# Placing the deferred layer-norm steps in ScalarE's order by a count of operands, in a two-layer graph kernel

## The chip, the cores and the metric

The kernel runs on one core of one Trainium2 chip. The metric is the device time of one execution in microseconds (us). The kernel before the change took 1790.8 us, the median of three runs (1789.74 to 1793.45); the execution that was profiled has a span of 1790.1 us.

In the text PE is TensorE (matrix products), DVE is VectorE, ACT is ScalarE, POOL is GpSimd, and SP is the engine whose queue issues the DMA transfers. [...]

## What is computed

There are 16 batches of a 1024 x 128 matrix x, one 1024 x 1024 matrix adj, and 128 x 128 (or 128 x 256) weights, all in float32. Two layers follow one another; each ends with a residual sum and a layer norm over the last axis.

```python
def layer0(x):                                  # a graph convolution
    return layernorm(x + adj @ (x @ w0) + b0)

def layer1(x):                                  # five steps of a gated graph network
    h = x
    for _ in range(5):
        m  = adj @ h                            # in and out matrix are both adj
        av = concat(m, m)
        u3 = h @ u3_w.T + u3_b
        z  = sigmoid(av @ w3_w.T + w3_b + u3)
        r  = sigmoid(av @ w4_w.T + w4_b + u3)
        hv = tanh(av @ w5_w.T + w5_b + (r * h) @ u5_w.T + u5_b)
        h  = (1 - z) * h + z * hv
    return layernorm(x + h)
```

Since both halves of `av` are the same, the two halves of each of w3, w4 and w5 are added once, and the sum is used as one 128 x 128 weight. These sums are the "weight sums" of the change.

## The kernel before

The batches are taken in four groups (q = 0 to 3) of four (k = 0 to 3). For each group, and in layer 1 for each of the five steps s, `aggregate` forms adj times the group by a two-level scheme of Strassen's kind (Winograd's form): seven outer products, each made of seven inner ones. The outer products are worked through in four **chains**, named after the outer products in them: 12, 3, 67 and 54. Chains 12, 67 and 54 handle two outer products side by side (two operands; `len(ns) == 2`), chain 3 only one. Every chain runs through its seven inner products in the order 1, 5, 6, 2, 7, 3, 4 (chain 54: 1, 5, 6, 2, 7, 3 first half, 4, 3 second half). After each inner product the result is taken out of PSUM by ACT or DVE:

```python
after = {
    1: lambda: nc.scalar.copy(fb, fa),               # pa -> pb, on ACT; product 6 goes on in pb
    5: lambda: nc.scalar.copy(x22, fc),
    6: lambda: nc.scalar.copy(x12, fb),
    2: lambda: nc.scalar.copy(x11, fa),
    7: lambda: nc.vector.tensor_add(x22, fb, x22),   # on DVE
    3: lambda: nc.vector.tensor_add(x12, fc, x12),
    4: lambda: nc.scalar.copy(x21, fb),
}
bank_of = {1: pa, 2: pa, 5: pc, 3: pc, 6: pb, 7: pb, 4: pb}
for item in order:
    for hook in hooks.get(item, ()):                 # other work, placed before this product
        hook()
    ...                                              # the matmuls of product a
    with tc.high_priority(), behind_closing():
        after[a]()
    drain(3 if len(ns) == 2 else 1)                  # L392
```

A layer norm takes its statistics on DVE, `rstd` and `shift` on POOL, and applies them on ACT, eight instructions of 128 x 128 for one batch. Those eight, and the transfer that stores the result, are not issued at once but put in a list. `drain` takes them off the list, after the inner products:

```python
def layernorm(y, tag, store, now=False):
    ...
    # 8 x bn_stats and 8 x bn_aggr on DVE                                  L246, L248
    nc.gpsimd.tensor_scalar(rstd, mv[:, :, 1], EPS, None, ALU.add)        # L251
    nc.gpsimd.tensor_tensor(rstd, rstd, power[:, :n], ALU.pow)            # L252
    nc.gpsimd.tensor_tensor(shift, mv[:, :, 0], rstd, ALU.mult)           # L253
    nc.gpsimd.tensor_scalar(shift, shift, -1.0, None, ALU.mult)           # L254

    def apply(c):
        return nc.scalar.activation(y[:, c, :], y[:, c, :], AF.Identity,  # L257
                                    bias=shift[:, c : c + 1], scale=rstd[:, c : c + 1])
    def put():
        nc.sync.dma_start(store, y)                                       # L263
    ...
    for c in range(n):
        waiting.append((slot[0], lambda c=c: tc.keep_in_program_order(apply(c))))
    waiting.append((slot[0], put))

waiting = deque()
slot = [0]

def drain(n, age=3):
    slot[0] += 1
    while waiting and n > 0 and slot[0] - waiting[0][0] >= age:
        waiting.popleft()[1]()
        n -= 1
```

Instructions under `tc.keep_in_program_order` keep the place in which the program states them; others are ordered by the compiler's scheduler, those under `tc.high_priority()` as early as they are ready there.

Layer norms arise in two places. In layer 0 the four norms of group q arise in chain 12 of the next aggregate, where `project(q, k, y)` multiplies the aggregate by w0. It first has ACT fill two PSUM tiles, `seeded`, with the bias (L448, kept in program order), then 16 matmul records per half on PE (L451), then the residual on DVE:

```python
def projections(q):
    room = rooms[q % 2]
    ys = [ypad[0], ypad[1], room[:, 2], room[:, 3]]
    for k in (2, 3):
        nc.sync.dma_start(ys[k], x_rows(q * QUAD + k))
    # before products 5, 2, 3 of chain 12, and at its end
    return {a: [call(project, q, k, ys[k])] for k, a in enumerate((5, 2, 3, "end"))}
```

At the end of chain 67, `fetch` flushes the list and loads the next group into the same buffers; the first sums over the next group (`ahead`) are placed at product 7 of chain 54. In group 1 the weight sums of layer 1 are placed at product 4 of chain 54:

```python
def fetch(q=q):
    drain(99, 0)
    for k in range(2):
        nc.sync.dma_start(ypad[k], x_rows(q * QUAD + k))
    if q + 1 < NQ:
        load(q + 1, rooms[(q + 1) % 2], x_rows)
    else:
        load(0, rows, saved_rows)
    ...
hooks.setdefault(67, {})["end"] = [fetch]
hooks[54] = {7: [call(ahead, rooms[(q + 1) % 2])]}
if q == 1:
    hooks[54][4] = [layer1_weights]
```

The first aggregate of layer 1 carries the projections of group 3 in the same way, with a flush before product 3 of chain 67 (`call(drain, 99, 0)`).

In layer 1 the closing norm of batch k of group q is taken in step k + 1 of group q + 1: `close` is placed before product 6 of chain 54 and works in the tile `hvs` (called `spare`). The next step's `next_load`, before product 1 of chain 3, loads other data into that tile. Chain 54 is followed at once by the **gates** (sigmoid, tanh, update), which need ACT for four instructions of 128 x 512 per unit. There are 12 such closings; the four batches of the last group are finished in `ending`, which flushes the list (`drain(99, 0)`) before each batch.

Of the kernel before, what the change touches and what calls it, by code (L numbers as in the profile page):

```python
# [20 lines left out]
def kernel(  # L21
# [73 lines left out]
    def bank(name, i=None):  # L95
        if i is None:
            i = turns[0]
            turns[0] = (i + 1) % 3
        return ps_m.tile([P, HALF], F32, tag=f"g{i}", name=name)
# [15 lines left out]
    def x_rows(b):  # L115
        return x[b].rearrange("(p c) d -> p (c d)", c=C)
# [91 lines left out]
    def layer0_weights():  # L208
        nc.sync.dma_start(w0_sb, w0)
        nc.sync.dma_start(b0_bc, bass.AP(tensor=b0.tensor, offset=b0.offset, ap=[[0, P], [1, D]]))  # L210

    raw_of = {
        "w3": (w3_w, hvs[:, 0, : 2 * D]), "w4": (w4_w, hvs[:, 0, 2 * D :]),
        "w5": (w5_w, hvs[:, 1, : 2 * D]), "u3": (u3_w, hvs[:, 1, 2 * D : 3 * D]),
        "u5": (u5_w, hvs[:, 1, 3 * D :]),
    }
# [7 lines left out]
    def layer1_weights():  # L224


        tc.keep_in_program_order(nc.vector.tensor_add(bz, bias[:, 0:1], bias[:, 3:4]))
        tc.keep_in_program_order(nc.vector.tensor_add(br, bias[:, 1:2], bias[:, 3:4]))
        tc.keep_in_program_order(nc.vector.tensor_add(bh, bias[:, 2:3], bias[:, 4:5]))
        for name, (w, raw) in raw_of.items():  # L230
            if w.shape[1] == 2 * D:
                tc.keep_in_program_order(
                    nc.vector.tensor_add(raw[:, :D], raw[:, :D], raw[:, D : 2 * D])
                )
            pt = bank(f"pt_{name}")
            tc.keep_in_program_order(nc.tensor.transpose(pt[:, :P], raw[:, :D], ident))
            nc.vector.tensor_copy(w_t[name], pt[:, :P])
# [46 lines left out]
    waiting = deque()  # L284
    slot = [0]

    def drain(n, age=3):
        slot[0] += 1
        while waiting and n > 0 and slot[0] - waiting[0][0] >= age:
            waiting.popleft()[1]()  # L290
            n -= 1
# [9 lines left out]
    def blocks_of(src, ns):  # L301

        if ns in ((1, 2), (3,)):
            v = src.rearrange("p b (h j x) -> p b h j x", h=2, j=2)
            if ns == (1, 2):
                return lambda j, k: v[:, k, :, j]
            return lambda j, k: v[:, 2 + k, 1:2, j]
        at = {(6, 7): slice(1, 3), (5, 4): slice(0, 4, 3)}[ns]
        return lambda j, k: tsum[:, at, k, ts(j, QT)]

    def sums_of(src, ns, pinned=False):
        t = inner[0 if ns in ((1, 2), (6, 7)) else 1]
        for op in inner_sums(blocks_of(src, ns), [t[:, i, : len(ns)] for i in range(4)]):
            if pinned:
                tc.keep_in_program_order(op)
        return op
# [16 lines left out]
    def behind_closing():  # L333

        return tc.issue_after(closed[0].ins) if closed[0] else nullcontext()

    def chain(tag, src, turned, ns, results, hooks, order=(1, 5, 6, 2, 7, 3, 4)):

        xs = blocks_of(src, ns)
        t = inner[0 if ns in ((1, 2), (6, 7)) else 1]
        w = len(ns) * QT
        right = {
            1: xs(0, 0), 2: xs(1, 0), 3: xs(1, 1), 4: t[:, 3], 5: t[:, 0], 6: t[:, 1], 7: t[:, 2],
        }

        def chunk(a, o, c):
            form = "p (d c) -> p c d" if turned else "p (c d) -> p c d"
            return right[a][:, o].rearrange(form, c=2)[:, c]  # L350

        def flat(t):
            return t[:, :w].rearrange("p (o q) -> p o q", o=len(ns))

        pa = ps_m.tile([P, HALF], F32, tag="a", name=f"pa_{tag}")
        pc = ps_m.tile([P, HALF], F32, tag="c", name=f"pc_{tag}")
        fa, fb, fc = flat(pa), flat(pb), flat(pc)

        x11, x12, x21, x22 = results(0, 0), results(0, 1), results(1, 0), results(1, 1)
        after = {  # L360
            1: lambda: nc.scalar.copy(fb, fa),  # L361
# [3 lines that stand above are left out]
            7: lambda: nc.vector.tensor_add(x22, fb, x22),  # L365
# [5 lines that stand above are left out]
            for hook in hooks.get(item, ()):  # L371
                hook()
            a, part = item if isinstance(item, tuple) else (item, range(len(ns)))
            for o in part:
                n = ns[o]
                for c in range(2):
                    product = nc.tensor.matmul(  # L377
                        bank_of[a][:, ts(o, QT)], chunk(a, o, c), left[n][a][:, c, :],
                        start=(a in (1, 5) and o == 0 and c == 0), stop=(c == 1),
                        skip_group_check=True,  # L380
                    )

                    if turned and a in (5, 6, 2) and ns in ((1, 2), (3,)) and o == c == 0:
                        tc.keep_in_program_order(product)

                    if item != a or (ns == (5, 4) and a == 4):
                        tc.keep_in_program_order(product)
            if o < len(ns) - 1:
                continue
            with tc.high_priority(), behind_closing():  # L390
                after[a]()
            drain(3 if len(ns) == 2 else 1)  # L392
        for hook in hooks.get("end", ()):
            hook()

# [234 lines left out]
    def call(f, *args):  # L630
        return lambda: f(*args)
# [9 lines that stand above are left out]
# [11 lines left out]
    for q in range(NQ):  # L652
        room = rooms[q % 2]
        hooks = {}
        if q == 0:
            hooks[12] = {
                5: [turn_rest],
                6: [outer_left, call(sums_of, rows, (3,))],
                7: [call(outer_sums, rows), call(inner_left, 6), call(inner_left, 7)],
            }  # L660
            hooks[67] = {1: [call(inner_left, 5), call(inner_left, 4)]}
            layer0_weights()
            with tc.issue_after(last_left.ins):
                sums_of(rows, (1, 2))
        else:
            hooks[12] = projections(q - 1)
            hooks[12][6] = [call(sums_of, room, (3,)), call(outer_sums, room, False, True)]
# [9 lines that stand above are left out]
            if q == 0:  # L677
                load_layer1_weights()

        def ahead(room):  # L680
            sums_of(room, (1, 2))
            outer_sums(room, True, False)

        hooks.setdefault(67, {})["end"] = [fetch]
        hooks[54] = {7: [call(ahead, rooms[(q + 1) % 2])]}
        if q == 1:
            hooks[54][4] = [layer1_weights]
        if q == 0:
            with tc.issue_after(last_left.ins):
                aggregate(f"x{q}", room, hooks, False)  # L690
        else:
            aggregate(f"x{q}", room, hooks, False)
# [71 lines left out]
    for q in range(NQ):  # L764
        for s in range(STEPS):
            tag = f"{q}_{s}"
            if s == 0:
                if q == 0:
                    hooks = {
                        12: projections(NQ - 1),  # L770
                        3: {5: [call(to_hidden, 0)], 2: [call(to_hidden, 1)]},
                        67: {
                            3: [call(drain, 99, 0), call(to_hidden, 2)],
                            "end": [call(to_hidden, 3)],
                        },
                        54: {},
                    }
                    hooks[12][6] = [call(sums_of, rows, (3,)), call(outer_sums, rows, False, True)]
                else:
                    outer_sums(rows)  # L780
                    hooks = {54: {}}
            else:
                hooks = {54: {}}
# [96 lines left out]
```

## Time and profile before

| what | value |
|---|---|
| time, median of three runs | 1790.8 us |
| span of the profiled execution | 1790.1 us |
| PE busy | 1768.5 us |
| DVE busy | 1309.0 us |
| ACT busy | 789.9 us |
| POOL busy | 94.3 us |
| one apply of a norm on ACT (128 x 128), median | 482 to 487 ns; 7 in a row take 2.80 us |
| ACT copy of a two-operand inner product (128 x 512) | 0.57 to 0.59 us |
| ACT copy of a one-operand inner product (128 x 256) | 0.37 us |
| `rstd` by `pow` on POOL (L252), median | 1.67 us |
| store of a normalized batch, issue to landing, median | 2.6 to 3.3 us |
| load of a batch, issue to landing, median | 3.6 to 4.1 us |

Groups of instructions are written as line, engine, operation, output<-inputs, shape, count, then busy time, mean of one and idle time of the engine ahead of them with what ended it ("<-"). In the timeline each row is a start, a length, an engine and an instruction; idle time ahead of it stands in brackets. A row in which PE is idle names what it waited for. In the table of stretches of time, each row gives the stretch, its length, the busy time of every engine with the number of instructions, the mean granted PE clock (1.00 is full speed), and the share and rate of the DMA engines.

### The profile page before, as it was taken

To read this page: it belongs to the slowest core of one execution; us is meant where nothing else is said; L and a number is where in the kernel's file an instruction comes from. 1 tells how busy PE (TensorE), PEld (TensorE's weight loads), DVE (VectorE), ACT (ScalarE), POOL (GpSimd) and SP (SyncE) were. 2 spreads that over 40 slices of the span, in tenths; PEclk is the share of its full clock that TensorE was granted. 3 is DMA by queue.
4 is the path that set the end of the run, shared out by engine and by line. 5 is a ranking of instruction groups with operands and counts; after the bars stand their busy time and mean duration, and the time that the engine had idled before them with its cause. 6 is when DMAs were issued, how large, how long until landed. Compare 5 with 4: busy or idle time off the path is not lost.

```text
span 1790.1 us, 19915 instructions
## 1 busy us (share of the span) xinstructions
PE 1768.5 (99%) x6709; PEld 1267.6 (71%) x6709; DVE 1309.0 (73%) x2280; ACT 789.9 (44%) x1418; POOL 94.3 (5%) x142
## 2 busy tenths in 40 slices
PE   8999999999999999999999999999999999999998
PEld 7788885857668586775857667585775857667584
DVE  7977786676767757777777857777777577777777
ACT  2345555253443534435253443534435253453536
POOL 0112220000000000000000000000000000000004
PEclk9999999999999999999999999999999999999999
DMA  6232344331414415252442415234143231514222
GB/s 226 71 118 106 130 114 96 74 85 33 112 30 94 118 36 118 56 133 57 97 97 92 106 36 118 71 86 115 52 114 106 48 80 50 118 36 95 71 71 94
DMA packets 404212, 159.25 MB, mean 89 GB/s; under 512 B 388240, under 2 KB 389136, under 8 KB 404112
## 3 DMA queue, kind: packets, MB, share of 16 engines
q1 hardware_dynamic: 403248, 154.84, 33.8%
q10 hardware_dynamic: 864, 3.15, 0.4%
q8 instruction: 54, 0.88, 0.2%
q14 instruction: 46, 0.38, 0.1%
HBM read 92.93 MB, written 65.01 MB: 88 GB/s over the span
## 4 chain that ended last, share of the span: by engine, by line
PE 93%; DVE 3%; POOL 1%; ACT 1%; issue 1%; DMA 0%; SPq 0%; DVEq 0%; POOLq 0%
PE pb L377 23%; PE pa L377 13%; PE pc L377 13%; PE ph L517 8%; PE pu L476 8%; PE pu L494 8%; PE seeded L509 8%; PE ph L518 8%; PE pa_x L377 2%; PE pc_x L377 2%; PE seeded L451 1%; POOL rstd L252 1%; ACT ypad L257 0%; DMA rows<-in_x_dram 0%; DVE stats L246 0%
## 5 line engine op out<-in xcount | busy, mean ns | idle before, releaser
L377 PE MATMUL pb<-e,inner 128*128 128x256 f32 x864 | 206.8, 380 | 3.0 <-ACT pb L361 3.0
L533 DVE TENSOR_TENSOR tsum<-tsum,hid 128x512 f32<-128x512 f32 x158 | 108.8, 689 | 107.7 <-ACT tsum L528 107.6
L377 PEld LDWEIGHTS pb<-e,inner 128*128 128x128 f32 x864 | 167.7, 195 | 23.1 <-ACT pb L361 5.0
L528 ACT ACTIVATE tsum<-ph,bh 128x512 f32<-128x512 f32 x158 | 108.5, 687 | 165.4 <-PE ph L518 165.4
L517 PE MATMUL ph<-agg,w_t 128*128 128x512 f32 x320 | 164.7, 596 | 0.0
L494 PE MATMUL pu<-agg,w_t 128*128 128x512 f32 x320 | 164.4, 595 | 0.1
L509 PE MATMUL seeded<-agg,w_t 128*128 128x512 f32 x320 | 163.5, 592 | 0.0
L518 PE MATMUL ph<-tsum,u_t 128*128 128x512 f32 x320 | 163.5, 592 | 0.0
L476 PE MATMUL pu<-hid,u_t 128*128 128x512 f32 x320 | 157.1, 592 | 0.0
L377 PE MATMUL pb<-s,inner 128*128 128x256 f32 x576 | 148.5, 381 | 0.2 <-DVE agg L365 0.2
L377 PE MATMUL pb<-a,inner 128*128 128x256 f32 x576 | 145.4, 381 | 0.0
L504 DVE TENSOR_TENSOR tsum<-tsum,hid 128x512 f32<-128x512 f32 x160 | 110.4, 690 | 46.4 <-ACT tsum L497 46.4
L497 ACT ACTIVATE tsum<-pu,br 128x512 f32<-128x512 f32 x160 | 109.8, 686 | 62.6 <-PE pu L494 62.6
L377 PE MATMUL pc<-e,inner 128*128 128x256 f32 x560 | 134.1, 379 | 0.0
L377 PEld LDWEIGHTS pb<-s,inner 128*128 128x128 f32 x576 | 110.3, 195 | 24.4 <-issue 9.9
L377 PEld LDWEIGHTS pb<-a,inner 128*128 128x128 f32 x576 | 112.3, 196 | 12.1
L512 ACT ACTIVATE tsum<-seeded,bz 128x512 f32<-128x512 f32 x160 | 109.7, 685 | 24.1 <-PE seeded L509 24.1
L377 PEld LDWEIGHTS pc<-e,inner 128*128 128x128 f32 x560 | 109.4, 196 | 11.7 <-issue 0.2
L517 PEld LDWEIGHTS ph<-agg,w_t 128*128 128x128 f32 x320 | 59.8, 190 | 78.2 <-issue 69.0
L518 PEld LDWEIGHTS ph<-tsum,u_t 128*128 128x128 f32 x320 | 61.0, 190 | 76.4 <-issue 57.5
L476 PEld LDWEIGHTS pu<-hid,u_t 128*128 128x128 f32 x320 | 61.0, 191 | 73.4 <-issue 72.3
L534 DVE TENSOR_TENSOR tsum<-tsum 128x512 f32<-128x512 f32 x158 | 109.2, 691 | 5.0
(180 smaller groups left out, 2855.9 us busy)
## 6 DMA issues: line engine op xcount, KB each, us to landing
turned<-ypad SPq DMA_DIRECT2D x48, 512.0 KB, 3.8
rows<-turned SPq DMA_DIRECT2D x192, 128.0 KB, 2.8
hvs<-saved SPq DMA_DIRECT2D x24, 512.0 KB, 3.9
rows<-saved SPq DMA_DIRECT2D x20, 512.0 KB, 4.1
hid<-hidden SPq DMA_DIRECT2D x64, 128.0 KB, 3.3
turned<-ypad SPq DMA_DIRECT2D x32, 256.0 KB, 2.9
rows<-turned SPq DMA_DIRECT2D x128, 64.0 KB, 2.1
hid<-in_x_dram SPq DMA_DIRECT2D x12, 512.0 KB, 3.9
```

Source lines behind the costliest of these rows:

```text
L377: product = nc.tensor.matmul(bank_of[a][:, ts(o, QT)], chunk(a, o, c), left[n][a][:, c, :], start=(a in (1, 5) and o == 0 and c == 0), sto ...
L476: in_order(nc.tensor.matmul(pu, w_t["u3"], hid[:, k, ts(h, HALF)], start=True, stop=True, skip_group_check=True))
L494: in_order(nc.tensor.matmul(pu, w_t["w4"], agg[:, k, cols], start=False, stop=True, skip_group_check=True))
L497: pin(nc.scalar.activation(rh[:, cols], pu, AF.Sigmoid, bias=br))
L504: pin(nc.vector.tensor_mul(rh[:, cols], rh[:, cols], hid[:, k, cols]))
L509: in_order(nc.tensor.matmul(pz, w_t["w3"], agg[:, k, cols], start=False, stop=True, skip_group_check=True))
L512: pin(nc.scalar.activation(z_of[k % 2][:, cols], pz, AF.Sigmoid, bias=bz))
L517: in_order(nc.tensor.matmul(ph, w_t["w5"], agg[:, k, cols], start=True, stop=False))
L518: in_order(nc.tensor.matmul(ph, w_t["u5"], rh_of[k % 2][:, cols], start=False, stop=True))
L528: pin(nc.scalar.activation(hv, ph, AF.Tanh, bias=bh))
L533: pinned(nc.vector.tensor_sub(hv, hv, hid[:, k, cols]))
L534: pinned(nc.vector.tensor_mul(hv, hv, z_of[k % 2][:, cols]))
```

## The change

Three things change. First, the age of a waiting step is counted in operands and not in calls: a product of a chain with two operands counts two, of chain 3 one, and a flush counts nothing. A step has to be fourteen behind its norm (seven products with two operands) and not three calls. Second, at most two steps are placed after a product with two operands, and not three; chain 3 keeps one. Both are meant to keep ACT from standing at a step whose `shift` POOL has not delivered, and from serving several steps ahead of a PSUM copy. Third, the weight sums on DVE are separated from the transposes that turn the weights on PE and placed earlier in chain 54, at its product 5, so that PE finds them done when it turns the weights at product 4.

```diff
-        for name, (w, raw) in raw_of.items():
+        for w, raw in raw_of.values():
             if w.shape[1] == 2 * D:
                 tc.keep_in_program_order(
                     nc.vector.tensor_add(raw[:, :D], raw[:, :D], raw[:, D : 2 * D])
                 )
+
+    def turn_weights():
+        for name, (_, raw) in raw_of.items():
             pt = bank(f"pt_{name}")
             tc.keep_in_program_order(nc.tensor.transpose(pt[:, :P], raw[:, :D], ident))
             nc.vector.tensor_copy(w_t[name], pt[:, :P])
...
-    def drain(n, age=3):
-        slot[0] += 1
+    def drain(n, age=14, time=0):
+        slot[0] += time
         while waiting and n > 0 and slot[0] - waiting[0][0] >= age:
             waiting.popleft()[1]()
             n -= 1
...
-            drain(3 if len(ns) == 2 else 1)
+            drain(2 if len(ns) == 2 else 1, time=len(ns))
...
         if q == 1:
-            hooks[54][4] = [layer1_weights]
+            hooks[54][5] = [layer1_weights]
+            hooks[54][4] = [turn_weights]
```

No instruction is added or removed; only places in the order change.

## The prediction

> **What bounds the kernel now.** I began with the page's busy times and its groups.
>
> ```profile
> PE 1768.5 (99%) x6709; PEld 1267.6 (71%) x6709; DVE 1309.0 (73%) x2280; ACT 789.9 (44%) x1418; POOL 94.3 (5%) x142
> PE 93%; DVE 3%; POOL 1%; ACT 1%; issue 1%; DMA 0%; SPq 0%; DVEq 0%; POOLq 0%
> ```
>
> PE is busy for all but 21.6 us of 1790.1, and the chain that ended last runs through PE for 93% of the span. A change that moves no PE work can win only PE's idle time and whatever PE loses by running slowly. So the ceiling comes first. I compared the starts of successive matmul records with the usual distance for their shape (216 ns for 128x256, 429 ns for 128x512, about 118 ns for 128x128, each the commonest in this trace). Added over the span, PE is late by some 30 us. About 15 of these lie in the first 60 us, ahead of any norm and out of reach. The last 8 us, after PE's last matmul, are out of reach too.
>
> Next I asked what ended ACT's idle time (columns: who <- for whom, total us, times, longest).
>
> ```profile
> ACT hvs L257 <- POOL shift L254: 18.0, 6, 3.1
> ACT ypad L257 <- POOL shift L254: 4.5, 4, 2.9
> ACT rows L257 <- POOL shift L254: 3.2, 1, 3.2
> ACT ypad L257 <- DVE stats L246: 2.6, 1, 2.6
> ```
>
> ACT stands at applies (L257) whose `shift` is not ready: an age of three products is too little, since POOL needs some 2.5 us more after DVE's statistics (75.83 to 78.42 us for one norm in the chain of waits). Whether PE suffers is seen only where it happens. In the timeline of group 1, chain 12 going over into chain 3:
>
> ```profile
> 84.89 0.58 ACT L367 COPY first<-pb 128x512 f32<-128x512 f32 x1 [2.21 <-PE pb L377]
> 88.35 0.49 ACT L257 ACTIVATE ypad<-ypad,shift,rstd 128x128 f32<-128x128 f32 x1 [2.88 <-POOL shift L254]
> 88.75 0.36 ACT L361 COPY pb<-pa_x 128x256 f32<-128x256 f32 x1
> 89.16 1.13 PE L377 MATMUL pb<-e,inner 128*128 128x256 f32 x4 [2.58 <-ACT pb L361]
> ```
>
> One apply waits 2.88 us for POOL; the copy that the next product in pb needs is placed behind it; PE is idle 2.58 us. In group 2 six applies stand ahead of the bias fill of `seeded`:
>
> ```profile
> 137.72 2.42 ACT L257 ACTIVATE ypad<-ypad,shift,rstd 128x128 f32<-128x128 f32 x6 [2.55 <-DVE stats L246]
> 140.05 1.08 ACT L448 COPY seeded<-b_bc 128x512 f32<-128x512 f32 x2
> 140.67 3.00 PE L451 MATMUL seeded<-w_sb,agg 128*128 128x128 f32 x16 [1.81 <-ACT seeded L448]
> ```
>
> Both gaps cost twice, as the table by stretches shows in its clock column (third from the right):
>
> ```profile
> 86.50:90.00 3.50, 0.92 (x5) 0.77 (x5) 3.44 (x9) 1.65 (x5) 3.17 (x5) 1.00 0.38 132
> 90.00:94.00 4.00, 4.00 (x21) 3.85 (x20) 0.69 (x1) 2.87 (x7) 1.92 (x3) 0.57 0.00 0
> 138.50:140.50 2.00, 0.37 (x2) 0.00 (x0) 1.75 (x4) 2.00 (x6) 1.26 (x2) 1.00 0.00 0
> 140.50:145.00 4.50, 4.33 (x20) 4.06 (x21) 1.91 (x6) 1.45 (x4) 1.73 (x3) 0.63 0.29 117
> ```
>
> After each gap PE is busy throughout, but at a clock of 0.57 and 0.63. The trace has the clock at one half for 3.41 us from 90.5 and again from 141.7, and at full speed everywhere else between 15 us and the end. Each costs half of 3.41, 1.7 us, which the busy times do not show.
>
> [...]
>
> **The change part by part.** I went through the list by hand for a layer-0 group with both rules (a two-operand product gives 2 counts, chain 3 gives 1).
>
> *Layer 0, age.* Before, the first applies of the norm made ahead of product 5 come at product 2 of the same chain, two products later. After, seven two-operand products must pass, and no apply is left in chain 12 at all: the first comes at product 5 of chain 3, when `shift` has been ready for over 10 us. So both gaps shown go, with their slow clock: group 1, 2.58 + 1.7 = 4.3 us; group 2, 1.81 + 1.7 = 3.5 us. Small delays beside them (0.2 to 0.3 us per group, after copies that applies held up) bring 0.5. In group 3 and in the first aggregate of layer 1 the six applies ahead of `seeded` cost PE about 0.5 us each, and a copy of pb behind three applies another 0.25 us: 1.5 together. Sum: 9.8 us.
>
> *At most two.* A two-operand product lasts 8 x 0.216 = 1.73 us. Three applies at 0.40 (2.80 us for seven) and a copy of 0.58 are 1.8 us; two are 1.4 us, so ACT keeps up. That is a safeguard; I count nothing for it.
>
> *Closings of layer 1.* Now the eight applies fall into the last three products of chain 54 and the first gates. In the trace of one of them ACT goes through 3 + 3 + 2 applies between sigmoids from 741.7 to 746.0, and PE's product at L517 starts 0.14 us late, and 0.10 us more passes before its next record. Over the 12 closings I find 0.17 to 0.25 us each that ACT causes: about 2.4 us. After, the steps become due at product 5 of the next chain 12, where ACT has 1.73 us per product for 1.4 us of work. The six waits of ACT for POOL (18.0 us) vanish as well, but they hardly held up PE and bring nothing more. Part of the delays (0.19 us in six closings) is DVE's, which still makes the statistics there; it stays.
>
> *Weight sums.* At 118.6 to 121.6 DVE adds the halves just ahead of each transpose; PE idles 0.58 us for the third and is late by about 1 us in all. Placed at product 5 the sums, three times 0.28 us plus three small ones, fit into DVE's idle 0.72 us at 113.5. Gain 0.8 us, once.
>
> Gain in sum: 9.8 + 2.4 + 0.8 = 13.0 us.
>
> **What it can cost.** Fewer steps per product and a later start mean that the list isn't empty when `fetch` comes: by my count 16 entries are left (14 applies, 2 stores), where before there were none; in layer 1's first aggregate the forced flush meets 20 (17 applies) and before 2. Fourteen applies take 5.6 us of ACT. They can be overtaken by the high-priority copies (88.75 above is such an overtaking), so that a copy waits for one apply at most, 0.48 us, and PE has a whole product, 1.73 us less a 0.58 us copy, to spare. But the last store, issued at 107.4 us before, moves to about 109.9 + 5.6 + three copies of 0.58 = 117 us. The load into the same buffer waits for it: [...] The trace shows this wait:
>
> ```profile
> 107.42 0.33 SPq L263 DMA_DIRECT2D saved<-rows  x1
> 110.86 0.33 SPq L113 DMA_DIRECT2D rows<-in_x_dram  x1
> 114.25 1.23 DVE L326 TENSOR_TENSOR tsum<-rows 128x1024 f32<-128x1024 f32 x1 [0.72 <-DMA rows<-in_x_dram]
> ```
>
> Store to load 3.4 us, load to first use 3.4 us. After, the load would land near 124 us instead of 114. PE doesn't need these rows before chain 3, some 20 us further on; but DVE takes its instructions in order, and in chain 12 it is full (20.01 us busy of the 21.00 from 69 to 90, 20.26 of 24.00 from 124 to 148). I estimate 0.5 to 1 us of new PE waits at each of the four seams: 3 us. Net: 13.0 - 3 = 10 us.
>
> **Rivals.** (1) *The load becomes the wait.* If the scheduler leaves L326 where it is in DVE's order, DVE stands up to 10 us, the sums for product 5 of chain 12 come late, and PE loses perhaps 6 us and 1.7 us of slow clock in each of three groups: 23 us, and a time of about 1800. Against it: DVE's order follows the scheduler's own forecast of when the load lands, and that forecast was only 0.7 us off at 114.25. (2) *DVE becomes the bound in chain 12.* With ACT's waits gone, PE needs about 20.7 us there (12 for seven products, 8.6 for four projections of 2.15), DVE 20. Then the gap of group 2 closes only in part: a net gain of some 6 us, 1785. (3) *Everything hidden.* The late stores and loads cost nothing: 1790.8 - 13 = 1778. (4) *The end.* The last closing's applies are now flushed into the gates of `ending`, 3.2 us in one lump ahead of tanh; PE can go on for about two products of 0.86 us in free PSUM banks there, so up to 1 us is lost.
>
> **Range and chances.** 1780.7 us is the sum. Below, the ceiling of 13 us and a run-to-run spread of some 2 us give 1776. Above, the second rival and part of the first give 1788.5. Faster by over 2% needs 36 us, more than PE's late time within reach; I give it 0.01. Slower by over 2% needs the first rival to be worse than estimated: 0.02.
>
> **What would show it.** Right: no apply between 69 and 90 us and in the later chains 12 of layer 0; PE's waits for `pb L361` and `seeded L448` gone; the clock at 1.00 throughout after 15 us; ACT's waits for `shift` near zero except at the end; 14 applies bunched after chain 67; PE's idle for `hvs L233` gone. Wrong: a new row of DVE waiting for `rows<-in_x_dram` or `rows<-saved` of over 2 us with a PE gap behind it; a half-speed stretch at a new place; closings in chain 12 that hold up the copy of pb, so that the steps of layer 1 get longer than the 76.6 us they take without a closing.

## The result and the profile after

The changed kernel takes 1778.5 us, the median of six runs (1777.9 to 1779.3), against 1792.1 us for the one before in the same number of runs (1789.0 to 1794.8). The ratio is 0.9924, with a 95% interval of 0.9911 to 0.9937: 13.6 us, or 0.8%, faster. Beside a later repetition of the changed kernel (1778.5 us) the kernel before took 1790.4 us, so the gain there was 11.9 us, and it is known to about 2 us. The prediction was 1780.7 us. The profiled execution has a span of 1776.1 us.

The page of the changed kernel, its rows of busy time and of the chain that ended last:

```profile
PE 1760.3 (99%) x6709; PEld 1263.2 (71%) x6709; DVE 1308.0 (74%) x2280; ACT 794.3 (45%) x1418; POOL 99.0 (6%) x142
PE 94%; DVE 3%; DMA 1%; POOL 0%; SPq 0%; issue 0%; ACT 0%; DVEq 0%
```

The counts are the same; only the order differs. PE is busy 8.2 us less for the same 6709 matmul records. That is not less work. In the two groups of layer 0 that held the half-speed stretches it is 4.5 us, of which the clock makes 3.4: at half speed the starts of 128x256 records lie 427 ns apart (before, from 143.9 us) and not 216, and the records count as busy throughout (3.42 of 3.42 us from 90.47 us on, at a clock of 0.50). Another 3.1 us lie in layer 1 between 775 and 1697 us, where the clock was full in both kernels. There records only started a little late, and a record of 128x512 lasts 0.59 us at a usual distance of 0.43 us, so that a short delay does not show as idle time. PE's idle time fell from 21.6 us to 15.8 us.

ACT's waits for POOL in the changed kernel (who <- for whom, total us, times, longest), where before there were three such rows with 25.7 us:

```profile
ACT rows L260 <- POOL shift L257: 3.2, 1, 3.2
```

The single wait left is the last norm of the kernel. (Lines are shifted: L257 before is L260 after, L448 is L451; in the kernels below with a list of ages L448 is L454.) In the timeline of ACT at the seam of chains 12 and 3 of group 1, which held the gap of 2.58 us before, the bias fill and the copy now come at once, and the first apply stands at product 5 of chain 3, as counted:

```profile
83.82 0.58 ACT L370 COPY first<-pb 128x512 f32<-128x512 f32 x1 [5.33 <-PE pb L380]
84.30 1.11 ACT L451 COPY seeded<-b_bc 128x512 f32<-128x512 f32 x2
85.34 0.35 ACT L364 COPY pb<-pa_x 128x256 f32<-128x256 f32 x1
87.57 0.37 ACT L365 COPY agg<-pc_x 128x256 f32<-128x256 f32 x1 [1.89 <-PE pc_x L380]
87.84 0.49 ACT L260 ACTIVATE ypad<-ypad,shift,rstd 128x128 f32<-128x128 f32 x1
```

The copy to pb starts at 85.34, and ACT waits for PE instead of the reverse. In the table by stretches for the same two places (clock third from the right), PE is busy throughout and the clock is full:

```profile
84.00:90.00 6.00, 6.00 (x36) 5.28 (x36) 5.79 (x35) 3.91 (x11) 4.31 (x6) 1.00 0.00 0
134.00:141.00 7.00, 7.00 (x41) 6.18 (x40) 6.71 (x41) 4.13 (x11) 2.61 (x6) 1.00 0.00 0
```

DVE is now nearly as full as PE there (5.79 of 6.00, 6.71 of 7.00 us). The starts of the same work in the two timelines show where the 14.0 us of the two spans come from ("gates" is the start of the first gate products, L476 before):

| point | before, us | after, us | difference | gained since the point above |
|---|---|---|---|---|
| group 1, first projection of group 0 | 69.35 | 68.60 | -0.7 | 0.7 |
| group 2, first projection | 126.11 | 119.59 | -6.5 | 5.8 |
| group 3, first projection | 180.90 | 170.19 | -10.7 | 4.2 |
| layer 1, first projection | 232.28 | 220.88 | -11.4 | 0.7 |
| layer 1, first gates | 276.84 | 264.99 | -11.8 | 0.5 |
| second step of layer-1 group 1, gates | 697.81 | 686.73 | -11.1 | -0.8 |
| last step, gates | 1697.50 | 1683.72 | -13.8 | 2.7 |
| end | 1790.1 | 1776.1 | -14.0 | 0.2 |

The first 0.7 us arise ahead of any norm and are chance: the first projection starts between 68.5 and 70.4 us in the thirteen profiles of this document. So about 11 us come from layer 0 and 3 to 4 from the closings in layer 1, less two losses near 399 and 706 us (0.8 and 0.7 us), of which more below.

### The profile page after: what moved, and what is told of

Its sections match the earlier page's. It is cut to its first block, busy times and chain, and to the rows that moved or that the text cites. A ratio compares the mean times of both kernels' runs of the same rounds, so it can differ in the third digit from the quotient of the medians.

```text
span 1776.1 us, 19907 instructions
## 1 busy us (share of the span) xinstructions
PE 1760.3 (99%) x6709; PEld 1263.2 (71%) x6709; DVE 1308.0 (74%) x2280; ACT 794.3 (45%) x1418; POOL 99.0 (6%) x142
## 4 chain that ended last, share of the span: by engine, by line
PE 94%; DVE 3%; DMA 1%; POOL 0%; SPq 0%; issue 0%; ACT 0%; DVEq 0%
PE pb L380 23%; PE pa L380 13%; PE pc L380 13%; PE pu L497 8%; PE seeded L512 8%; PE pu L479 8%; PE ph L521 7%; PE ph L520 7%; PE pc_x L380 2%; PE pa_x L380 2%; PE seeded L454 2%; DMA rows<-turned 1%; DMA rows<-in_x_dram 1%; DMA turned<-ypad 0%; SPq L573 0%
## 5 line engine op out<-in xcount | busy, mean ns | idle before, releaser
L380 PE MATMUL pb<-a,inner 128*128 128x256 f32 x576 | 143.9, 379 | 0.0
L380 PEld LDWEIGHTS pb<-s,inner 128*128 128x128 f32 x576 | 110.2, 194 | 25.7 <-issue 10.1
```

The source lines that it names most:

```text
L380: product = nc.tensor.matmul(bank_of[a][:, ts(o, QT)], chunk(a, o, c), left[n][a][:, c, :], start=(a in (1, 5) and o == 0 and c == 0), sto ...
```

## The experiments

Each was timed in five or more runs beside the kernel before. The ratio is to the kernel before, with its 95% interval.

**1. POOL's latency alone.** The theory is A: ACT waits for POOL's `shift`, and PE for ACT. Its rival is B: ACT is overloaded by applies placed ahead of copies, whatever POOL does. In this kernel the inverse square root is left out and nothing moves; the order on all five engines is that of the kernel before.

```diff
-        nc.gpsimd.tensor_tensor(rstd, rstd, power[:, :n], ALU.pow)
+        nc.gpsimd.tensor_tensor(rstd, rstd, power[:, :n], ALU.mult)
```

> The kernel before, with the pow on POOL (L252) replaced by a multiplication of the same operands; it leaves out the inverse square root, so its output is not the layer norm's. The order of instructions is that of the kernel before on every engine. Theory A (POOL's latency is what ACT and then PE wait for): the norm's POOL chain gets about 1.4 us shorter, PE's gap of 2.58 us in group 1 shrinks to about 1 us and that of 1.81 us in group 2 to under 0.5, the half-speed stretches behind them go, and the time falls by 5 to 8 us without any instruction having moved. Rival B (ACT is simply overloaded by applies placed ahead of copies, whatever POOL does): the gaps stay above 1.5 us and the time falls by less than 2 us.

Measured: 1783.1 us, ratio 0.9962 (0.9948 to 0.9975), 7.5 us by the medians. ACT's timeline at the seam of group 1:

```profile
86.48 0.49 ACT L257 ACTIVATE ypad<-ypad,shift,rstd 128x128 f32<-128x128 f32 x1 [0.94 <-POOL shift L254]
86.88 0.36 ACT L361 COPY pb<-pa_x 128x256 f32<-128x256 f32 x1
```

and PE's, and the stretches there:

```profile
87.29 1.13 PE L377 MATMUL pb<-e,inner 128*128 128x256 f32 x4 [0.65 <-ACT pb L361]
```

```profile
86.50:90.00 3.50, 2.85 (x19) 2.48 (x19) 3.50 (x11) 3.50 (x9) 2.06 (x3) 1.00 0.35 137
90.00:94.00 4.00, 4.00 (x23) 3.54 (x22) 3.17 (x14) 2.18 (x7) 0.31 (x2) 1.00 0.20 81
```

ACT's wait fell from 2.88 to 0.94 us, PE's gap from 2.58 to 0.65, and the clock stayed full. The `pow` took 1.67 us of POOL, the multiplication 0.20. ACT's order shows here too: the copy at 86.88 stands behind the apply and starts after it. Rival B falls for the two large gaps in layer 0. From the first projection to the first gates this kernel gains 8.1 us, without any instruction moved. What is left of rival B is what stays: 0.3 to 0.7 us of PE gap in a group. From the first gates to the last ones the kernel gained only 0.7 us more, although ACT's waits for `shift` in the closings (`hvs`) fell from 18.0 to 9.2 us: POOL is the smaller part of what the closings of layer 1 cost.

**2. The three parts one by one.** `e_age` is the first part alone:

```diff
-    def drain(n, age=3):
-        slot[0] += 1
+    def drain(n, age=14, time=0):
+        slot[0] += time
-            drain(3 if len(ns) == 2 else 1)
+            drain(3 if len(ns) == 2 else 1, time=len(ns))
```

> The kernel before with the first part alone: age counted in operands, fourteen, but still three steps per product with two operands, and the weight sums where they were. Theory A: the age carries nearly all of the gain, so 11 to 13 us less than before. Rival B (the limit of two is what frees ACT): 5 us less or under that.

`e_two` is the second part alone:

```diff
-            drain(3 if len(ns) == 2 else 1)
+            drain(2 if len(ns) == 2 else 1)
```

> The kernel before with the second part alone: two steps per product with two operands, age still three calls. Theory A: the waits for shift remain, since the first applies keep their place at product 2, so within 2 us of before; at most the six applies ahead of seeded become four and the gaps there shrink by 0.8 us each. Rival B: 5 us less or more than that.

`e_sums` is the third part alone: `layer1_weights` split, its sums at product 5 and `turn_weights` at product 4 of chain 54, as in the diff of the change.

> The kernel before with the third part alone: the weight sums at product 5 of chain 54, the transposes at product 4, norms as before. Both theories: PE's waits for hvs near 120 us go, 0.8 to 1.0 us less than before, once; the gaps of groups 1 and 2 with their half-speed stretches stay.

| kernel | median, us | ratio, interval |
|---|---|---|
| age alone | 1779.0 | 0.9942 (0.9929 to 0.9954) |
| limit of two alone | 1790.5 | 1.0001 (0.9993 to 1.0009) |
| weight sums alone | 1789.4 | 0.9995 (0.9987 to 1.0003) |
| kernel before beside them | 1790.6 | |

The age carries the gain, 11.6 us by the medians. The limit alone changes nothing measurable. In its profile it loses 0.9 us up to the first gates and wins 2.3 us in the closings, where by the count six applies instead of eight now come before the step's end; that this is the reason was not shown. The sums alone are within the spread of the runs, but their profile shows the expected 0.8 us: PE's waits for `hvs` are gone.

The kernel of the weight sums also shows what the slow clock costs. Its gap in group 1 is the same as before the change, to 0.01 us (PE's timeline):

```profile
88.33 1.13 PE L380 MATMUL pb<-e,inner 128*128 128x256 f32 x4 [2.59 <-ACT pb L364]
```

but the clock does not fall behind it, only behind the gap in group 2 (why is not shown; what was measured of it stands in the last section):

```profile
89.00:93.00 4.00, 4.00 (x28) 3.66 (x27) 1.49 (x3) 3.62 (x11) 2.09 (x3) 1.00 0.00 0
138.00:143.00 5.00, 5.00 (x23) 4.45 (x22) 3.52 (x18) 1.79 (x5) 0.86 (x3) 0.66 0.38 134
```

From the first projection of group 1 to that of group 2 this kernel takes 54.2 us (68.52 to 122.74), the one before 56.8: 2.5 us less, of which 0.8 are the sums and 1.7 the half-speed stretch that did not come.

**3. How old a step must be.** In layer 0 the age is eight, twelve or twenty-eight; layer 1 keeps fourteen.

```diff
-    def drain(n, age=14, time=0):
+    ages, most = [8], [2]                # [12] in e_twelve, [28] in e_late
+    def drain(n, age=None, time=0):
+        age = ages[0] if age is None else age
...
+            if (q, s) == (0, 1):         # second step of layer 1
+                ages[0], most[0] = 14, 2
```

> The changed kernel with an age of eight in layer 0 (four products with two operands): two applies each come at products 7, 3 and 4 of chain 12 again, ahead of the bias fills of the third and fourth projection, but with shift ready by then. Theory A (it is the wait for POOL that costs, not an apply ahead of a copy): within 1.5 us of the changed kernel, no gap over 1 us in chains 12. Rival B (applies ahead of the pinned fills cost by themselves): 3 us or more slower, with gaps before seeded.

> The changed kernel with an age of twelve in layer 0. With eight, shift came 2.65 us after the apply was due; twelve counts are two products, 3.5 us, more, so shift should be ready, and the list left for the flush is shorter. If POOL's wait is all that the age must cover: within 1.5 us of the changed kernel. If an apply ahead of the bias fill costs by itself, or the scheduler's order of DVE at the seams is as sensitive as with three steps: 2 us or more slower.

> The changed kernel with an age of 28 in layer 0 (layer 1 keeps fourteen): 30 entries, 26 of them applies, are left for the flush at the end of chain 67 instead of 16 and 14. The last store then lands some 5 to 7 us later, and with it the load of the next group. Theory A (copies overtake the applies, and the scheduler moves DVE's sums behind the later load): the same time as the changed kernel within 1.5 us. Rival C (the prediction's 3 us of seam costs are real and were made good elsewhere; the load becomes the wait): 4 us or more slower than the changed kernel, with DVE waiting for rows<-in_x_dram over 2 us and PE gaps behind it.

| age in layer 0 | median, us | ratio, interval |
|---|---|---|
| 8 | 1791.9 | 1.0005 (0.9997 to 1.0012) |
| 12 | 1779.7 | 0.9941 (0.9929 to 0.9954) |
| 14, the changed kernel repeated | 1778.5 | 0.9930 (0.9916 to 0.9943) |
| 28 | 1788.4 | 0.9988 (0.9982 to 0.9995) |

With eight the whole gain of layer 0 is lost and more (the closings still gain 3.3 us in its profile), against what I had expected. My step "shift ready by then" failed. ACT's timeline in group 2:

```profile
134.39 0.88 ACT L260 ACTIVATE ypad<-ypad,shift,rstd 128x128 f32<-128x128 f32 x2 [2.65 <-POOL shift L257]
135.18 1.09 ACT L454 COPY seeded<-b_bc 128x512 f32<-128x512 f32 x2
```

and PE's:

```profile
135.81 2.15 PE L457 MATMUL seeded<-w_sb,agg 128*128 128x128 f32 x16 [2.10 <-ACT seeded L454]
```

The norm's bias fill started at 121.59 and its `shift` was ready at 134.36 us. DVE finished the statistics only at 131.57, because it serves the next projection in between; POOL then takes 2.7 us. So a step must wait for a DVE that is full, not for POOL alone, and ages of twelve and fourteen cover that where eight doesn't. The 3 us or more of rival B came, but not by its mechanism: the gap follows a wait for `shift`.

With twelve no apply waits for `shift` in layer 0, and the kernel is 1.2 us above the changed one, within the 1.5 us expected. Its profile does show a small cost of an apply ahead of a bias fill by itself: three of the projections start 0.37 us late, where those of the changed kernel start 0.10 us late.

With twenty-eight I was wrong in the other direction: 9.9 us slower than the changed kernel. DVE's waits for the loads did not grow; rival C fell with its mechanism, but so did "copies overtake". The loss sits in two places. At three chains 67 the order on PE itself changed, so that the first half of product 2 stands directly behind product 1 and is 0.88 us late each time; for two of the three the profile names the copy of product 1, for the third a sum on DVE. And at the seam from layer 0 to layer 1 the flush stands ahead of the copies (ACT's timeline):

```profile
263.93 6.25 ACT L260 ACTIVATE hid<-hid,shift,rstd 128x128 f32<-128x128 f32 x16
270.08 0.56 ACT L368 COPY rows<-pc 128x512 f32<-128x512 f32 x1
```

PE's timeline there:

```profile
271.18 1.13 PE L383 MATMUL pb<-s,inner 128*128 128x256 f32 x4 [3.04 <-ACT rows L369]
```

Sixteen applies in a row, no copy among them, and PE idle 3.04 us. In the changed kernel the same seam has at most eight in a row, and PE does not wait. With 1.2 us more at the same seam (255.79 us) and 0.5 us at 194.09, these late starts come to 7.6 us. The profiled span of this kernel, 1783.3 us, lies 7.2 us above the changed kernel's; its other runs show a lower mean clock than the profiled one (0.996 to 0.998, against 0.999). By an estimate from the traces, one half-speed stretch lowers the mean by 0.001 (half of 3.41 us in 1783) and costs 1.7 us, so one or two more of them in those runs would account for the remaining 2.7 us; that they occurred there is not shown.

**4. The closings alone.** From the second step of layer 1 on the old rule holds, in its new terms:

```diff
+            if (q, s) == (0, 1):
+                ages[0], most[0] = 6, 3
```

> The changed kernel, but from the second step of layer 1 on with the old rule in its new terms (six counts, that is three products with two operands; three steps per product), so that the twelve closings fall on chain 54 and the first gates as before. Theory A: the changed kernel gains about 3.2 us by the closings (read from the starts of the steps in the two traces, from -11.1 at the second step of group 1 to -13.8 us at the last one, where two late DVE sums gave back some) and the rest in layer 0; so this one is 2.5 to 3.5 us slower than the changed kernel and about 10.5 us faster than the one before. Rival B (the closings cost nothing, since PE is fed either way): within 1 us of the changed kernel.

Measured: 1782.4 us, ratio 0.9950 (0.9937 to 0.9963), 3.8 us above the changed kernel's median. Its steps grow against those of the repeated changed kernel by 0.2 to 0.7 us at nearly every closing, 3.7 us by the end (spans of 1780.0 and 1776.4 us). So rival B of this run, that the closings cost nothing, falls, and the cost is a little above the 2.5 to 3.5 us expected. Here the applies hold up ACT's other work for the most part by their place, as rival B of experiment 1 had it: eight of them stand between sigmoids, and a shorter POOL won back only 0.7 us. One closing of the kernel before, in DVE's timeline:

```profile
973.78 0.69 DVE L504 TENSOR_TENSOR tsum<-tsum,hid 128x512 f32<-128x512 f32 x1 [2.94 <-ACT tsum L497]
974.39 1.29 DVE L434 TENSOR_TENSOR agg<-rows 128x512 f32<-128x512 f32 x2
```

and in ACT's:

```profile
971.92 1.26 ACT L257 ACTIVATE hvs<-hvs,shift,rstd 128x128 f32<-128x128 f32 x3 [2.98 <-POOL shift L254]
973.09 0.67 ACT L497 ACTIVATE tsum<-pu,br 128x512 f32<-128x512 f32 x1
```

DVE waits for a sigmoid that stands behind three applies, the first of which waited for `shift`, and the sums that PE needs (L434) stand behind that on DVE.

**5. The limit of two beside the age.** `e_three` puts three steps per product back in the whole changed kernel; `e_split` only from the second step of layer 1 on; `e_ctrl` is the changed kernel unaltered.

```diff
-            drain(2 if len(ns) == 2 else 1, time=len(ns))
+            drain(3 if len(ns) == 2 else 1, time=len(ns))    # e_three
```

> The changed kernel with three steps per product with two operands again. PE's and POOL's order is that of the changed kernel; on ACT the list is shorter by the time of the flush. Theory A (the limit is a safeguard that costs and brings nothing): within 1 us of the changed kernel. Rival D (three applies and a copy, 1.8 us, are more than the 1.73 us of a product, so copies come late): 1.5 us or more slower.

> The changed kernel with two steps per product in layer 0 and three from the second step of layer 1 on. If the limit matters only through the order that it gives DVE at the seams of layer 0 (with three, the sum over the next group was placed ahead of work that PE needed, and waited 3.1 us for its load), this one is as fast as the changed kernel within 0.7 us, and chain 12 of layer 1 shows three applies and a copy per product without a PE gap.

> The changed kernel once more, unaltered, beside the two below on the same chip. In its first profile two sums on DVE waited 1.6 us for rows<-turned in steps of layer 1 that hold no norm (near 399 and 706 us) and cost PE 1.5 us together; DVE's order there is the same in the kernel with three steps per product, whose profile has no such wait. If this is luck in when the transfers land, they are absent or elsewhere here and the span is up to 1.5 us shorter; if it belongs to the order, they come back at the same places.

| kernel | median, us | ratio, interval |
|---|---|---|
| three steps everywhere | 1779.6 | 0.9937 (0.9925 to 0.9949) |
| three in layer 1 only | 1777.7 | 0.9931 (0.9919 to 0.9944) |
| changed kernel repeated | 1778.5 | 0.9930 (0.9916 to 0.9943) |

By their times the three can't be told apart. Their profiles can: that of three steps everywhere is 1.9 us later than that of the repeated changed kernel in layer 0. With three everywhere, DVE's timeline at the seam of groups 1 and 2:

```profile
118.04 1.23 DVE L329 TENSOR_TENSOR tsum<-rows 128x1024 f32<-128x1024 f32 x1 [3.14 <-DMA rows<-in_x_dram]
119.18 0.68 DVE L369 TENSOR_TENSOR hid<-pc_x,hid 128x512 f32<-128x512 f32 x1
```

and PE's waits:

```profile
PE pc_x L380 <- DVE hid L369: 1.5, 1, 1.5
```

This is the first rival of the prediction, the load that becomes the wait, on a small scale: the scheduler put the sum over the next group ahead of L369, DVE took the two in that order (3.14 us of waiting, the sum at 118.04, L369 at 119.18), and PE is 1.7 us late. The reason that rival D gave, copies that come late behind three applies, is not what is seen. In the changed kernel (DVE's timeline) the same sum stands behind it and waits 0.44 us:

```profile
117.45 0.68 DVE L369 TENSOR_TENSOR hid<-pc_x,hid 128x512 f32<-128x512 f32 x1
118.05 1.28 DVE L437 TENSOR_TENSOR agg<-hid 128x512 f32<-128x512 f32 x2
119.78 1.23 DVE L329 TENSOR_TENSOR tsum<-rows 128x1024 f32<-128x1024 f32 x1 [0.44 <-DMA rows<-in_x_dram]
```

In layer 1 three applies and a copy per product leave PE without a gap (16.00 us busy of 16.00 from 764 to 780 us in `e_split`), so the limit isn't needed there once the age is fourteen. The two losses near 399 and 706 us are absent from the repeated run of the same kernel: they were luck in when `rows<-turned` landed and no part of the change. No version was found that is measurably faster than the changed kernel.

## Why the prediction was right, and where its terms were off

The result, 1778.5 us, lies in the range of 1776 to 1788.5 and 2.2 us below the point.

- **PE is the bound, and only its late time can be won: right.** PE's records were late by 30.5 us in sum before and 16.6 us after, by the same count of starts. The difference is that of the spans. By this count 12.0 us lay in the first 60 us, not the 15 that were said to be out of reach, so 18.5 us were within it; 5.3 of these are left.
- **Layer 0, age, 9.8 us, with the sums 10.6: right.** The table of starts gives 11.1 from the first projection to the first gates. Experiment 1 shows that the wait for `shift` caused most of it, 8.1 us; experiment 2 that the age removes it. The last 2 us are argued: experiment 1 left a wait of 0.94 us, and applies still stood ahead of copies.
- **Each gap costs twice: right in size, but not always so.** The 1.7 us for a half-speed stretch was in the profile I read. The same gap without it (experiment 2) shows that it can stay away, so the 3.4 us counted for the two hold for that profile and not for every run of the kernel before.
- **At most two, nothing: right in time, incomplete in reason.** The limit wins about 2 us in the closings if they stay in the gates (one profile), and in layer 0 it decides where the scheduler puts a DVE sum.
- **Closings, 2.4 us: too small.** The runs of experiment 4 show 3.7. The step that failed is "part of the delays is DVE's, which still makes the statistics there; it stays". It was ACT's as well, by way of a sigmoid for which DVE waited. And the six waits for `shift`, said to bring nothing more, stood ahead of such sigmoids: a shorter POOL alone brought 0.7 us in the closings.
- **Weight sums, 0.8 us: right** by the profile of `e_sums`; the timing alone can't show it. The fit into 0.72 us did not add up (three times 0.28 is already 0.84), and the sums went elsewhere: in the changed kernel they take 0.9 us at 108.1, ahead of 3.6 us in which DVE waits for ACT.
- **Costs at the seams, 3 us: the largest miss.** They were near zero. The step that failed is the one from a late load to a DVE that stands: DVE waited 0.44 us. The load's sum came at 119.8 us, which is early by the clock only because PE was ahead by then; against the group's first projection (126.1 before, 119.6 after) it moved from 11.9 us ahead to 0.2 us behind, later than the estimate of 124 us, which would have been 2.1 us ahead. DVE lost nothing because the scheduler had put other work ahead of it (L369 and L437, experiment 5), which is what the prediction held against its first rival. ACT did not hold up PE either (ACT's timeline of the flush, changed kernel):

```profile
104.46 1.65 ACT L260 ACTIVATE rows<-rows,shift,rstd 128x128 f32<-128x128 f32 x4
106.00 0.58 ACT L364 COPY pb<-pa_x 128x512 f32<-128x512 f32 x1
```

The scheduler had put the copies between the applies, three or four of these at a time, as the prediction said it could. The experiments with three steps, and with an age of 28, show that the fear was well founded: both the late load and the lump ahead of copies appear as soon as the order shifts a little. That neither appeared at fourteen and two was in part luck: the prediction had no count that tells these values from their neighbours.
- **DVE as the bound in chain 12 (second rival): not yet.** It is at 96% of the stretches shown, and PE doesn't wait for it.
- **The end (fourth rival): no loss seen.** From the last gates to the end the changed kernel takes 92.4 us, the one before 92.6.

Net: 13.0 us predicted as gain and 3 as cost; 13.6 us found by the medians (11.9 in the repetition), with no cost at the seams of layer 0 to set against them. From the first projection on, the profile of the repetition is 14.7 us shorter than that of the kernel before: 11.1 in layer 0 and 3.6 after it.

## What to carry to other kernels

Deferring work by a fixed number of calls is a guess at a latency; count in units of time, and take the latency from the trace, from the first instruction of the producer to the last, with the queueing on a full engine in it. An engine's share does not tell whether it holds up the one that bounds the kernel: ACT, 44% busy over the span, took the copy at 88.75 us behind an apply that had waited 2.88 us, and PE was idle for 2.58: look at what stands ahead of the urgent instructions of such an engine, not at its share. After such a change, test ages on either side, since too late a place (9.9 us at an age of 28) costs nearly as much as too early a one (13.4 us at eight).

## What the runs showed of the hardware

Some gaps of PE were followed by a half-speed stretch and some were not. In the kernel before, those of 2.58 us in group 1 and 1.81 us in group 2 were each followed by one: 3.41 us at a clock of 0.50, from 90.47 and from 141.68 us. The length of the gap alone does not decide: in the kernel with the weight sums alone, the gap of 2.59 us in group 1 was not followed by one (1.00 from 89 to 93 us), although one came in group 2 (0.66 from 138 to 143 us), where PE was idle for 1.82 of the 3 us ahead of it.

The trace of the kernel before shows how the stretches lie. They start at 11.97, 90.47, 141.68 and 1786.90 us; the distances are 23, 15 and 482 times 3.4133 us, and the first three stretches last 3.413 us each. The 3.41 us that ended where the first stretch of group 1 began, in the kernel before:

```profile
87.06:90.47 3.41, 1.31 (x6) 1.08 (x7) 2.88 (x5) 2.12 (x6) 3.08 (x5) 1.00 0.27 108
```

and two such lengths over which the equal gap of the kernel with the weight sums fell, counted back from its own stretch in group 2 (by that count at 138.61 us, 15 lengths after 87.41):

```profile
84.00:87.41 3.41, 1.74 (x9) 1.19 (x7) 3.41 (x21) 0.59 (x1) 2.76 (x4) 1.00 0.50 147
87.41:90.82 3.41, 2.49 (x16) 2.26 (x17) 1.70 (x2) 3.31 (x9) 3.17 (x4) 1.00 0.02 7
```

In the first, PE was idle for 2.10 of 3.41 us; in the other two for 1.67 and 0.92. Ahead of the stretch at 141.68 us of the kernel before it was idle for 1.81 (138.26 to 141.67 us). My estimate from these spacings and idle times is that a gap of some 2 us brought the slow clock or not by where it fell between such starts; what decides was not shown. The kernel before spreads over 5.8 us from run to run (1789.0 to 1794.8) and the changed one, whose profile has no such gaps, over 1.4; that half-speed stretches make this difference is not shown either, since the single runs' traces are not on record.
